# Two cross-attention layers: one after the other, or in common slots twelve tiles apart

## The chip, the cores and the metric

The kernel runs on one core of a Trainium2 chip. A core has a matrix engine (TensorE, PE in the profile; PEld is its weight load), a vector engine (VectorE, DVE), an engine for activation functions (ScalarE, ACT), a general engine (GpSimd, POOL) and a synchronization engine (SyncE, SP) that here issues all the DMAs. Each engine works through its own queue in order; semaphores make one engine wait for another. Operands lie in an on-chip memory of 128 partitions (SBUF), products of TensorE in a second one (PSUM). The metric is the device time of one execution in microseconds (us), the median of several runs.

## The reference

The input x has 4 batches of 1024 rows with 256 features; the context has 4 batches of 77 rows. Four layers follow each other. Layers 0 and 1 are the same in both kernels and are left out here. Layers 2 and 3 are attention from the rows of x to the 77 rows of the context, with 16 heads:

```python
# layer 2 (queries = x, keys = values = context)
q, k, v = heads(queries @ Wq.T + bq), heads(keys @ Wk.T + bk), heads(values @ Wv.T + bv)
scores = einsum('bhqd,bhkd->bhqk', q, k) / sqrt(16)
scores = where(attention_mask, -inf, scores * attention_weights)
out = einsum('bhqk,bhkd->bhqd', softmax(scores), v)
x = queries + heads_joined(out) @ Wo.T + bo
x = (x - mean(x)) * rsqrt(var(x) + 1e-5) * gamma + beta
# layer 3 (hidden_states = x, key_value_states = context)
normed = x * rsqrt(mean(x * x) + 1e-6) * norm_w
q, k, v = heads64(normed @ wq), heads64(context @ wk), heads64(context @ wv)
attn = softmax(einsum('bhqd,bhkd->bhqk', q, k))
x = x + heads64_joined(einsum('bhqk,bhkd->bhqd', attn, v)) @ wo
```

`attention_weights` and `attention_mask` are inputs of 4 x 16 x 1024 x 77, so that each tile of rows has its own. Layer 3 of a row needs layer 2 of that row alone: the rows do not mix in these two layers. All is float32.

## The kernel before, in words

x lies in SBUF for the whole kernel, as 4 batches (NB) of 8 tiles (NT) of 128 rows: 32 tiles. A row of scores has 16 heads x 77 keys = 1232 values (HK), or ten chunks of 128 columns (NC).

The order of the work is written out by hand: the program lists instructions, and each engine's queue holds its own in the order of the program. Software pipelining is therefore also written out: a *slot* i works on several tiles at once, each at a different step.

Layer 2, `slot2(i)` (line 1457), touches tile i and the tiles 1, 3, 4 and 5 before it. In order of the program: the sixteen exponentials of tile i-1 (ACT, L1473); the scores of tile i (PE, L51, `ps<-kb,qT`), their product with the attention weights (DVE, L1485) and the masked entries put to a low value (DVE, L1490); the output product of tile i-5 (PE, `po2`); the product of weights and values of tile i-4 (PE, `pvT`) and its copy `oT` (ACT, L1507); the maxima of tile i (DVE, L1510, scaled in L1514); the turning of the weights of tile i-3 (PE transposes, L1375, ten chunks in three groups, each followed by an ACT copy into `pT`, L1376); the addition of the output of tile i-5 to x (DVE, L1520; the bias on POOL, L1521); and last the sums of tile i-1 (DVE, L1526, L1527) and the division of its weights by them (POOL, L1528). The attention weights and the mask of tile i+1 are loaded into a `side` buffer, of which there are two, when slot i begins (SP, L1453, L1454).

Layer 3, `slot3(i)` (L1571), has its queries and keys folded into one matrix `G` per batch, and its values and output weights into one matrix `U` per batch, both computed much earlier and kept in DRAM. It touches tile i and tile i-2: in two halves, the turning of tile i-2 and the scores of tile i from `G` (PE), the maxima and the subtraction (DVE, L1599, L1600); then one exponential (ACT, L1608), the sums (DVE, L1611, L1612), the division (POOL, L1613); then the output of tile i-2 from `U` (PE), its addition to x (DVE, L1623) and its store (SP, L1624).

All 32 slots of layer 2 come first, then all 32 of layer 3; the five slots that empty the pipeline of layer 2 are laid into the first five of layer 3. Work that belongs to a batch and not to a tile runs as a *job*, a generator that is advanced a little at two places of each slot (`gap2`), by shares that `jobs2` and `jobs3` write down:

- `prep2(b)` makes the queries of layer 2: 16 transposes, copies, 16 products, biases.
- `norm2(b)` is the layer norm that ends layer 2: statistics (DVE), `inv_std` with a power on POOL (L293), the norm (ACT, L1543), gamma and beta (POOL, L1546, L1547).
- `stats3(b)` and `features3(b)` are the root-mean-square norm of layer 3: statistics, `inv_std`, the normed rows `xn` (DVE, L316), their transposes `ptx` (PE, L339) and `xT` (DVE, L345).
- `loads2(b)` loads the values `V` of layer 2, `loads3(b)` the matrices `G` (L1567) and `U` (L1398, L1401) of layer 3.
- `combine1` finishes the last batch of layer 1.

Buffers tie queues together: a load into a buffer waits until the last reader of what lay there is done, and it waits at the head of SP's queue, ahead of all the loads behind it. `U` and `V` share one pair of buffers, `pT` has three, the weights `s` have four, the PSUM pool for outputs (`po2`, `po3`) has one buffer, the small PSUM pool `sm` (transposes, values, query products) three, the pool for scores two.

Of the kernel before, what the change touches and what calls it, by code (L numbers as in the profile page):

```python
# [17 lines left out]
P = 128  # L18
# [9 lines left out]
SC = 0.25  # L28
# [3 lines left out]
def tile_xattn_seq(ctx: ExitStack, tc: tile.TileContext, d: dict, out: bass.AP):  # L32
# [252 lines left out]
    def inv_std(rs, mv, eps, rms):  # L285

        if rms:
            nc.gpsimd.tensor_tensor(rs, mv[:, :, 0], mv[:, :, 0], ALU.mult)
            nc.gpsimd.tensor_tensor(rs, rs, mv[:, :, 1], ALU.add)
            nc.gpsimd.tensor_scalar_add(rs, rs, eps)  # L290
        else:
            nc.gpsimd.tensor_scalar_add(rs, mv[:, :, 1], eps)
        nc.gpsimd.tensor_tensor(rs, rs, nhalf, ALU.pow)  # L293
# [1084 lines left out]
    def new_scores():  # L1378
        s = late.tile([P, P * NC], F32, name="s", tag="s", bufs=4)
        nc.gpsimd.memset(s[:, HK:], 0.0)  # L1380
        return s
# [11 lines left out]
    def load_folded(b):  # L1393

        U = late.tile([P, NC, D], F32, name="U3", tag="qu")
        rows_of_u = kept_u[b].rearrange("h s n -> (h s) n")
        n = P * (NC - 1)
        nc.sync.dma_start(  # L1398
            out=U[:, 0 : NC - 1, :], in_=rows_of_u[0:n].rearrange("(c p) n -> p c n", p=P)
        )  # L1400
        nc.sync.dma_start(out=U[0:HSIZE, NC - 1, :], in_=rows_of_u[n:HK])  # L1401
        return U

    def loads2(b):

        V = late.tile([P, NC, D], F32, name="V2", tag="qu").rearrange("p c n -> p (c n)")
        V = V[:, 0 : (NC + 1) * P].rearrange("p (c n) -> p c n", n=P)
# [18 lines left out]

    def prep2(b):

        x = xs[b]
        xT = late.tile([P, 2, T], F32, name="xT2", tag="xT")  # L1430
        yield from to_features(xT, lambda i: x[:, i, :], None, None, None, None)
        qT = late.tile([P, 2, T], F32, name="qT2", tag="gs")
        for o in range(2):
            for q in range(2):
                pp = sm.tile([P, 512], F32, name="pp2", tag="sm")
                for c in range(2):
                    mm(
                        pp, l2["Wq"][:, c, P * o : P * o + P], xT[:, c, 512 * q : 512 * q + 512],
# [6 lines left out]
                if o and q:  # L1445
                    shared["b2", b] = qT
                yield

    def load_sides(i):
        b, t = divmod(i, NT)  # L1450
        side = late.tile([P, HK + HK // 4], F32, name="side", tag="side")
# [5 lines left out]
    def slot2(i, tiles, at, gap2):  # L1457


        p1, p3, p4, p5 = (tiles.get(i - k) for k in (1, 3, 4, 5))  # L1460
        a = None
        if i < NB * NT:
            b, t = divmod(i, NT)
            a = tiles[i] = dict(b=b, t=t)
            qT, kb = shared["b2", b], shared["k2"]
            fs, mk = shared.pop(("side", i))
            if i + 1 < NB * NT:
                load_sides(i + 1)
            s = a["s"] = new_scores()
        if p1:  # L1470
            for h in range(H):
                hs = p1["s"][:, S * h : S * h + S]
                nc.scalar.activation(hs, hs, AF.Exp, bias=p1["nm"][:, h : h + 1], scale=SC)  # L1473
        if a:
            for o in range(2):
                ps = pair_tile()
                for e in range(2):
                    r = half_rows(e)
                    mm(
                        ps[:, e, 0 : 4 * S].rearrange("p (h s) -> p h s", s=S),  # L1480
                        qT[r, o, P * t : P * t + P],
                        kb[r, o, :, b, :],
                    )
                so = slice(o * HH * S, (o + 1) * HH * S)
                nc.vector.tensor_tensor(  # L1485
                    s[:, so].rearrange("p (i n) -> p i n", i=2), ps[:, :, 0 : 4 * S],
                    fs[:, so].rearrange("p (i n) -> p i n", i=2), ALU.mult,
                )
            sv = s[:, 0:HK]
            nc.vector.copy_predicated(sv, mk, low.to_broadcast([P, HK]))  # L1490
        gap2(at + 0.4)
        if p5:
            xt = xs[p5["b"]][:, p5["t"], :]
            po = pvp.tile([P, D], F32, name="po2", tag="pv")
            for o in range(2):
                mm(po, p5["oT"][:, o, :], l2["Wo"][:, o, :], start=(o == 0), stop=(o == 1))
            del tiles[i - 5]
        if p4:

            V = shared["v2", p4["b"]]  # L1500
            pv = sm.tile([P, 2, P], F32, name="pvT", tag="sm")
            for k in range(NC + 1):
                o, c = (0, k) if k < 5 else (1, k - 1)
                r = slice(0, rows_in(c))
                mm(pv[:, o, :], V[r, k, :], p4["pT"][r, c, :], start=k in (0, 5), stop=k in (4, NC))
            oT = p4["oT"] = late.tile([P, 2, P], F32, name="oT", tag="oT")
            nc.scalar.copy(oT, pv)  # L1507
        if a:
            nm = a["nm"] = small.tile([P, H], F32, name="nm", tag="m16")
            nc.vector.tensor_reduce(  # L1510
                nm, sv.rearrange("p (h k) -> p h k", k=S), axis=AX.X, op=ALU.max
            )

            nc.vector.tensor_scalar(nm, nm, 0.1 * NEG, -SC, ALU.max, ALU.mult)  # L1514
        if p3:
            pT = p3["pT"] = late.tile([P, NC, P], F32, name="pT", tag="pT", bufs=3)
            for g in range(3):
                turned(p3["s"], g, pT)
        if p5:
            nc.vector.tensor_tensor(xt, po, xt, ALU.add)  # L1520
            nc.gpsimd.tensor_tensor(xt, xt, rows["bo"], ALU.add)  # L1521
        gap2(at + 1.0)
        if p1:
            s3 = p1["s"][:, 0:HK].rearrange("p (h k) -> p h k", k=S)
            den = small.tile([P, H], F32, name="den", tag="den")
            nc.vector.tensor_reduce(den, s3, axis=AX.X, op=ALU.add)  # L1526
            nc.vector.reciprocal(den, den)  # L1527
            nc.gpsimd.tensor_tensor(  # L1528
                s3, s3, den.unsqueeze(2).to_broadcast([P, H, S]), ALU.mult
            )  # L1530

    def norm2(b):

        x = xs[b]
        res = []
        yield from stats_job(res, lambda t: x[:, t, :], 1e-5, False)
        mv, rs = res
        away = small.tile([P, NT], F32, name="away", tag="away")
        nc.gpsimd.tensor_tensor(away, mv[:, :, 0], rs, ALU.mult)
        nc.gpsimd.tensor_scalar(away, away, -1.0, None, ALU.mult)  # L1540
        for t in range(NT):
            xt = x[:, t, :]
            nc.scalar.activation(  # L1543
                xt, xt, AF.Identity, bias=away[:, t : t + 1], scale=rs[:, t : t + 1]
# [3 lines left out]
            yield  # L1548


    def stats3(b):

        res = shared["st3", b] = []
        yield from stats_job(res, lambda t: xs[b][:, t, :], 1e-6, True)

    def features3(b):

        xT = shared["xT3", b] = late.tile([P, 2, T], F32, name="xT3", tag="xT")
        rs = shared["st3", b][1]
        yield from to_features(  # L1560
            xT, lambda t: xs[b][:, t, :], None, rs, cols["L3_xattn_norm_w"], None
        )

    def loads3(b):

        G = late.tile([P, 2, 8, 2, S], F32, name="G3", tag="gs")
        nc.sync.dma_start(  # L1567
            out=G.rearrange("p c f e s -> p (c f e) s"),
            in_=kept_g.rearrange("p c f e (b s) -> p (c f e) b s", s=S)[:, :, b, :],
        )  # L1570
        shared["b3", b] = (G.rearrange("p c f e s -> p c (f e s)"), load_folded(b))  # L1571
        yield

    def slot3(i, tiles, at, gap2):
        a, p2 = None, tiles.get(i - 2)
        if i < NB * NT:
            b, t = divmod(i, NT)
            a = tiles[i] = dict(b=b, t=t)
            G, _ = shared["b3", b]
            xT = shared["xT3", b]  # L1580
            s = a["s"] = new_scores()
            m = small.tile([P, H], F32, name="m3", tag="m16")
        if p2:
            pT = late.tile([P, NC, P], F32, name="pT", tag="pT", bufs=3)
        for o in range(2):
            if p2:
                turned(p2["s"], o, pT)
            if a:
                ps = pair_tile()
                for e in range(2):  # L1590
                    k0 = (2 * o + e) * 4 * S
                    for c in range(2):
                        mm(
                            ps[:, e, 0 : 4 * S], xT[:, c, P * t : P * t + P],
                            G[:, c, k0 : k0 + 4 * S], start=(c == 0), stop=(c == 1),
                        )
                pv = ps[:, :, 0 : 4 * S].rearrange("p i (h s) -> p i h s", s=S)
                mo = m[:, HH * o : HH * o + HH].rearrange("p (i h) -> p i h", i=2)
                nc.vector.tensor_reduce(mo, pv, axis=AX.X, op=ALU.max)  # L1599
                nc.vector.tensor_tensor(  # L1600
# [271 lines left out]
```

## Time and profile before

| | |
|---|---|
| time, median of 3 runs | 2310.22 us (2309.99 to 2316.91) |
| profiled execution, its own time | 2315.16 us |
| span of the profiled execution | 2313.4 us |
| mean granted clock of TensorE | 0.981 |
| TensorE busy | 2167.0 us (94%) |
| VectorE busy | 1511.2 us (65%) |
| ScalarE busy | 1028.1 us (44%) |
| POOL busy | 642.4 us (28%) |
| first score of layer 2 | at 1723.3 us |
| first score of layer 3 | at 1982.3 us |

The profile is of one execution. An engine's busy time is the time in which it ran instructions; register and semaphore instructions and the issue of DMAs are not counted. A line of the timeline has a start, a length, the engine, the line of the kernel, the operation, the tile that is written and those that are read, the shapes, the number of equal instructions in a row, and in brackets how long the engine had been idle before and which engine and tile released it. All matrix products have line 51, that of a helper, so that they are told apart by their tiles. Products on TensorE overlap: the cost of one is better read from the distance to the next start than from its length. The clock that TensorE was granted stands as a part of full speed.

### The profile page before, as it was taken

The page shows a single profiled execution, that of the slowest core. Times are in us where ns is not written, and L with a number is a line of the kernel's source. Part 1 is how long each engine was busy: PE and PEld are TensorE (multiplying, and loading weights), DVE is VectorE, ACT ScalarE, POOL GpSimd, SP SyncE. Part 2 cuts the span into 40 slices and gives each one's busy share as a digit, 9 for nine tenths or more (in the row PEclk, how much of TensorE's full clock was granted, in tenths as well). Part 3 has the DMA queues.
Part 4 walks back from the last instruction along what each step waited for, and adds up shares of the span by engine and source line. Part 5 has one row for each costly group of instructions (what it writes and reads, how often), then busy time and mean ns, then how long its engine had stood idle before and what let it go on. Part 6 is the DMA issues. An engine that isn't in the chain of part 4 may idle for free.

```text
span 2313.4 us, 41275 instructions
## 1 busy us (share of the span) xinstructions
PE 2167.0 (94%) x16874; PEld 1357.5 (59%) x16874; DVE 1511.2 (65%) x2492; ACT 1028.1 (44%) x1700; POOL 642.4 (28%) x927
## 2 busy tenths in 40 slices
PE   4999999999999999999989999999999998999999
PEld 2544444555555455554556675656556776788887
DVE  3756567755566555754376666777759999677664
ACT  1144444434444444344533444545548876432222
POOL 2011113111131112310152232333423655542221
PEclk9899999999999999999989999999999999999999
DMA  7221121100000000101000011101023334102200
GB/s 216 55 57 68 32 64 41 40 6 15 7 15 2 10 11 6 38 1 19 6 15 6 15 28 19 21 15 21 15 78 124 114 109 126 47 15 58 58 14 17
DMA packets 87858, 93.98 MB, mean 41 GB/s; under 512 B 35714, under 2 KB 77558, under 8 KB 87542
## 3 DMA queue, kind: packets, MB, share of 16 engines
q1 hardware_dynamic: 87670, 91.35, 15.1%
q8 instruction: 133, 2.18, 0.4%
q14 instruction: 55, 0.45, 0.1%
HBM read 55.31 MB, written 18.39 MB: 32 GB/s over the span
## 4 chain that ended last, share of the span: by engine, by line
PE 70%; DVE 14%; ACT 5%; issue 1%; POOL 1%; DVEq 0%; ACTq 0%
PE ps L51 27%; PE po L51 13%; PE pv L51 6%; PE pp L51 6%; PE ph L51 4%; DVE mpart L672 3%; PE psT L1375 2%; DVE ms L1138 2%; PE ppv L51 2%; PE pvT L51 2%; PE pvw L51 1%; DVE mrow L1142 1%; PE ptx L339 1%; PE pm L590 1%; PE pt L607 1%
## 5 line engine op out<-in xcount | busy, mean ns | idle before, releaser
L51 PE MATMUL ps<-qk 32*128 32x192 f32 (+9 forms) x6528 | 581.9, 428 | 57.8 <-DVE mpart L672 25.0
L738 ACT ACTIVATE pe<-ps 128x1024 f32<-128x1024 f32 (+2 forms) x384 | 363.3, 952 | 589.5 <-PE ps L51 581.5
L51 PEld LDWEIGHTS ps<-qk 32*128 32x128 f32 (+1 forms) x6528 | 315.9, 185 | 295.8 <-issue 75.5
L672 DVE TENSOR_REDUCE mpart<-ps 128x2 f32<-128x1024 f32 (+4 forms) x384 | 330.9, 884 | 241.9 <-PE ps L51 241.2
L741 POOL TENSOR_SCALAR_AFFINE_SELECT pe<-pe 128x256 f32<-128x256 f32 (+1 forms) x192 | 94.9, 495 | 665.5 <-ACT pe L738 664.6
L1214 ACT ACTIVATE pew<-ps 128x768 f32<-128x768 f32 x128 | 103.4, 812 | 196.4 <-PE ps L51 196.3
L1219 POOL TENSOR_SCALAR_AFFINE_SELECT pew<-pew 128x512 f32<-128x512 f32 x128 | 81.7, 638 | 338.0 <-ACT pew L1214 337.9
L1376 ACT COPY pT<-psT 128x512 f32<-128x512 f32 (+1 forms) x192 | 92.3, 518 | 175.4 <-PE psT L1375 174.9
L1138 DVE TENSOR_TENSOR ms<-ps,maskw 128x768 f32<-128x768 f32 x128 | 122.1, 954 | 69.7 <-PE ps L51 68.2
L51 PE MATMUL pv<-pe,va 128*32 128x512 f32 (+3 forms) x1536 | 157.1, 496 | 0.0
L51 PE MATMUL ph<-yT,w 128*128 128x256 f32 x512 | 143.1, 401 | 2.4 <-DVE va L401 1.0
L51 PE MATMUL po<-U,pT 128*128 128x256 f32 (+1 forms) x640 | 143.7, 379 | 0.2
L51 PE MATMUL ps<-G,xT 128*128 128x308 f32 x512 | 143.0, 423 | 0.0
L51 PEld LDWEIGHTS po<-w,hT 128*128 128x128 f32 x800 | 111.6, 192 | 47.7 <-issue 38.9
L1473 ACT ACTIVATE s<-s,nm 128x77 f32<-128x77 f32 x512 | 131.2, 347 | 17.3 <-DVE nm L1514 17.2
L51 PE MATMUL po<-w,hT 128*128 128x128 f32 (+1 forms) x800 | 138.0, 317 | 0.9 <-ACT hT L904 0.9
L665 DVE TENSOR_REDUCE mpart<-ps 128x8 f32<-128x1024 f32 x64 | 78.2, 1225 | 82.6 <-PE ps L51 82.4
L1613 POOL TENSOR_TENSOR s<-s,den 128x1232 f32<-128x1232 f32 x32 | 71.9, 2248 | 203.4 <-DVE den L1612 176.9
L51 PEld LDWEIGHTS po<-U,pT 128*128 128x128 f32 (+1 forms) x640 | 119.2, 190 | 15.5 <-ACT pT L1376 0.6
L51 PEld LDWEIGHTS ph<-yT,w 128*128 128x128 f32 x512 | 88.7, 192 | 63.9 <-issue 50.8
L1142 DVE TENSOR_REDUCE mrow<-ms 128x4 f32<-128x768 f32 x128 | 122.2, 955 | 4.4
L1375 PE MATMUL psT<-ident,s 128*128 128x128 f32 x640 | 92.9, 274 | 16.8 <-ACT oT L1507 13.0
(200 smaller groups left out, 3381.9 us busy)
## 6 DMA issues: line engine op xcount, KB each, us to landing
side<-in_fside_t SPq DMA_DIRECT2D x32, 616.0 KB
qk<-st SPq DMA_DIRECT2D x256, 64.0 KB
side<-in_mask_t SPq DMA_DIRECT2D x32, 154.0 KB
G<-kept_g SPq DMA_DIRECT2D x4, 1232.0 KB
U<-kept_u SPq DMA_DIRECT2D x4, 1152.0 KB
x<-in_x SPq DMA_DIRECT2D x8, 512.0 KB
out<-x SPq DMA_DIRECT2D x32, 128.0 KB
kept_g<-st SPq DMA_DIRECT2D x22, 154.0 KB
```

What stands on the lines that cost most here:

```text
L51: nc.tensor.matmul(o, lhsT, rhs, start=start, stop=stop, **kw)
L665: nc.vector.tensor_reduce(mpart[self.own][:, :, 2 * p : 2 * p + 2, 0].rearrange("p t j -> p j t"), ps.rearrange("p j (t n) -> p j t n", n= ...
L672: nc.vector.tensor_reduce(mpart[bl][:, i, 2 * p : 2 * p + 2, ci], ps[:, :, o : o + w], axis=AX.X, op=ALU.max,)
L738: nc.scalar.activation(pp[:n, :, o:512], ps[:n, :, o:512], AF.Exp, scale=SC)
L741: nc.gpsimd.affine_select(out=own, in_=own, compare_op=ALU.is_ge, fill=0.0, base=0, pattern=[[0, 2], [0, k], [1, P]], channel_multiplier=-1,)
L1138: nc.vector.tensor_tensor(v, ps.rearrange("p j (i n) -> p j i n", i=2)[:, :, :, 0:n], (maskw[:, 1:2] if w else maskw).unsqueeze(1).to_broa ...
L1142: nc.vector.tensor_reduce(mo, v, axis=AX.X, op=ALU.max, negate=True)
L1214: nc.scalar.activation(pp[:, :, :, 0 : P + WIN], ps.rearrange("p j (i n) -> p j i n", i=2)[:, :, :, 0 : P + WIN], AF.Exp, scale=SC,)
L1219: nc.gpsimd.affine_select(out=pf[:, :, 0:P], in_=pf[:, :, 0:P], compare_op=ALU.is_ge, fill=0.0, base=0, pattern=[[0, 4], [1, P]], channel_ ...
L1375: nc.tensor.transpose(ps[:, k, :], s[:, P * c : P * c + P], ident)
L1376: nc.scalar.copy(pT[:, 4 * group : 4 * group + n, :], ps[:, 0:n, :])
L1473: nc.scalar.activation(hs, hs, AF.Exp, bias=p1["nm"][:, h : h + 1], scale=SC)
```

## The change

Layers 2 and 3 run in common slots. `slot23(i)` takes the place of `slot2` and `slot3`: slot i works on layer 2 of tile i and on layer 3 of tile i-12 (`LAG`). There are 46 slots: slots 0 to 11 have layer 2 alone, in the order that `slot2` had; slots 12 to 36 have both; slots 37 to 45 have layer 3 alone, in the order that `slot3` had, but for the sums and the division, which are issued one slot later, after the first half of the scores.

A common slot is ordered so (c: tile of layer 3, c1 and c2 the ones before; p1, p3, p4, p5: tiles of layer 2, one to five before): turning of c2; four exponentials of p1; scores of layer 2; sums and division of c1; four exponentials; `more()`; output of c2; four exponentials; maxima; values of p4; `more()`; the last four exponentials; scores of layer 3; `more()`; turning of p3; exponential of c; sums of p1; output of p5 and its addition; `more()`; division of p1.

`more()` takes the place of `gap2`: it advances every job that is alive by a fixed number of steps, one for `combine1` and `prep2`, two or four for `between`. `between(g)` takes the place of `norm2`, `stats3` and `features3`: for four tiles it runs the layer norm of layer 2, the root-mean-square statistics, the normed rows and their transposes, in some 20 steps. It starts at slot 9 + 4g. `prep2` works in two halves of 512 rows, its copies are on ACT, and `prep2(b+1)` starts in slot 8b + 4. `loads2(b+1)` and `loads3(b)` are issued, whole, ahead of slot 8b + 4.

Buffers: `G`, `U` and `V` have two each of their own; `pT` becomes `pT2` and `pT3` with one each; `s` becomes `s2` with four and `s3` with two; the queries, half the transposed rows and `xT3` take places of weights that are no longer used.

The core of the diff, with the jobs:

```diff
-    def slot2(i, tiles, at, gap2):
-    def slot3(i, tiles, at, gap2):
...
+    def turned_x(dst, rows, g):
+
+        for c in range(2):
+            pt = sm.tile([P, 4, P], F32, name="ptx", tag="sm")
+            for i in range(4):
+                nc.tensor.transpose(pt[:, i, :], rows[i][:, c * P : (c + 1) * P], ident)
+            src = pt.rearrange("p i n -> p (i n)")
+            if g is None:
+                nc.scalar.copy(dst[:, c, :], src)
+            else:
+                nc.vector.tensor_scalar(dst[:, c, :], src, g[:, c : c + 1], None, ALU.mult)
+            yield
+
...
+    def stats4(st, mv, rs, g, eps, rms):
+
+        b, t0 = divmod(4 * g, NT)
+        for k in range(4):
+            nc.vector.bn_stats(st[:, k], xs[b][:, t0 + k, :])
+            nc.vector.bn_aggr(mv[:, k], st[:, k])
+            if k == 3:
+                inv_std(rs, mv, eps, rms)
+            yield
+        yield
+
+    def between(g):
+        b, t0 = divmod(4 * g, NT)
+        x = xs[b]
...
+        yield from stats4(st, mv, rs, g, 1e-5, False)
+        away = late.tile([P, 4], F32, name="away", tag="away")
+        nc.gpsimd.tensor_tensor(away, mv[:, :, 0], rs, ALU.mult)
+        nc.gpsimd.tensor_scalar(away, away, -1.0, None, ALU.mult)
+        yield
+        for k in range(4):
+            xt = x[:, t0 + k, :]
+            nc.scalar.activation(
+                xt, xt, AF.Identity, bias=away[:, k : k + 1], scale=rs[:, k : k + 1]
+            )
+            nc.gpsimd.tensor_tensor(xt, xt, rows["gamma"], ALU.mult)
+            nc.gpsimd.tensor_tensor(xt, xt, rows["beta"], ALU.add)
+            yield
...
+        yield from stats4(st, mv, rs, g, 1e-6, True)
+        xn = []
+        for k in range(4):
+            xt = small.tile([P, D], F32, name="xn", tag="xn", bufs=4)
+            normed(xt, x[:, t0 + k, :], None, rs, k)
+            xn.append(xt)
+            if k % 2:
+                yield
+        xT = shared["xT3"][:, g % 2]
+        yield from turned_x(xT, xn, cols["L3_xattn_norm_w"])
+        shared["ready3"] = g
+
+    LAG = 12
...
+        elif i < n + 5:
+            if c2:
+                turned_into(c2, "pT3")
+            if p1:
+                exps2(p1, range(4))
+            if a:
+                score2(a, i)
+            if c1:
+                sums_of(c1, "den3")
+                divided(c1)
+            if p1:
+                exps2(p1, range(4, 8))
+            more()
+            if c2:
+                out3(c2)
+            if p1:
+                exps2(p1, range(8, 12))
+            if a:
+                maxima2(a)
+            if p4:
+                values_of2(p4)
+            more()
+            if p1:
+                exps2(p1, range(12, H))
+            if c:
+                score3(c, j)
+            more()
+            if p3:
+                turned_into(p3, "pT2")
+            if c:
+                exp3(c)
+            if p1:
+                sums_of(p1, "den2")
+            if p5:
+                out2(p5)
+                add2(p5)
+            more()
+            if p1:
+                divided(p1)
...
-    run(slots(slot3, 2, jobs3, slots(slot2, 5, jobs2)))
...
+    for i in range(NB * NT + LAG + 2):
+        b, k = divmod(i, NT)
...
+        if k == 4:
+            if b + 1 < NB:
+                run(loads2(b + 1))
+            if b < NB:
+                run(loads3(b))
+        if k == 4 and b + 1 < NB:
+            live2.append((prep2(b + 1), 1))
+        if i >= 9 and (i - 9) % 4 == 0 and (i - 9) // 4 < NB * NT // 4:
+            live2.append((between((i - 9) // 4), 2 if i < 33 else 4))
+        slot23(i, two, three, more)
```

## The prediction

> **What bounds the kernel now.** I read the chain that ended last first (TensorE 70% of it), then the busy time by stage from the first score of layer 2 (1723.3 us) to the end, where all of the change lies: 590.1 us. Columns: window, its length, busy time (and instructions) per engine, granted clock, DMA share, GB/s.
>
> ```profile
> core 0: us, PE busy (x) PEld busy (x) DVE busy (x) ACT busy (x) POOL busy (x), PEclk, DMA share, GB/s
> 1723.30:1810.20 86.90, 79.45 (x504) 59.42 (x504) 82.92 (x106) 67.18 (x226) 28.90 (x29) 1.00 0.36 117
> 1810.20:1982.30 172.10, 149.28 (x964) 118.95 (x963) 157.86 (x239) 133.39 (x445) 105.81 (x126) 0.92 0.34 106
> 1982.30:2313.40 331.10, 325.83 (x1624) 267.19 (x1622) 210.88 (x330) 97.03 (x148) 101.56 (x103) 1.00 0.13 36
> ```
>
> Layer 2 (first two rows) is held by VectorE (157.9 of 172.1), layer 3 by TensorE (325.8 of 331.1). That is what common slots could use: together the stages ask 554.6 of TensorE, 451.7 of VectorE. So at best 590.1 − 554.6 = 35.5 us can be won. Next, the pitch of a tile, from starts of POOL's divisions (start, length):
>
> ```profile
> 1773.89 2.25 POOL L1528 TENSOR_TENSOR s<-s,den 128x1232 f32<-128x1232 f32 x1 [0.96 <-DVE den L1527]
> 1780.55 2.25 POOL L1528 TENSOR_TENSOR s<-s,den 128x1232 f32<-128x1232 f32 x1 [0.97 <-DVE den L1527]
> ...
> 2289.50 2.25 POOL L1613 TENSOR_TENSOR s<-s,den 128x1232 f32<-128x1232 f32 x1 [7.24 <-DVE den L1612]
> 2299.07 2.25 POOL L1613 TENSOR_TENSOR s<-s,den 128x1232 f32<-128x1232 f32 x1 [7.24 <-DVE den L1612]
> ```
>
> A slot of layer 2 with no job takes 6.65, one of layer 3 9.57 (6.65 is VectorE's work, 9.57 TensorE's). TensorE's work comes from the distances of starts in its timeline:
>
> ```profile
> 1771.19 1.31 PE L51 MATMUL ps<-kb,qT 64*128 64x308 f32 x8
> 1772.43 1.13 PE L51 MATMUL po<-w2q,oT 128*128 128x256 f32 x4
> 1773.40 2.62 PE L51 MATMUL pvT<-pT,V 128*128 128x128 f32 x22
> 1775.85 1.26 PE L1375 MATMUL psT<-ident,s 128*128 128x128 f32 x10
> ...
> 2104.09 2.24 PE L51 MATMUL ps<-G,xT 128*128 128x308 f32 x8
> ...
> 2108.90 4.49 PE L51 MATMUL po<-U,pT 128*128 128x256 f32 x20
> ```
>
> Layer 2: scores 1.05, output .86, values 2.45, turning 1.08 = 5.45 (each less what the next overlaps). Layer 3: scores 4.15, output 4.33, turning 1.08 = 9.56. A common slot costs TensorE 15.0. VectorE: 6.65 + 5.25 (max, subtract, sums, add) + a quarter of `between` (eight statistics of .53, four normed rows of .3, two `xT` of .75 = 7.0 per four tiles) = 13.7. So TensorE would be the bound of an undisturbed common slot, by 1.3 us.
>
> **What a late producer costs.** Waits of TensorE in layer 2 (total, times, longest), then one of them and the clock behind it:
>
> ```profile
> PE psT L1375 <- ACT oT L1507: 13.0, 6, 4.2
> PE ptx L339 <- DVE xn L316: 2.7, 2, 2.5
> ```
> ```profile
> 1833.83 0.69 PE L1375 MATMUL psT<-ident,s 128*128 128x128 f32 x2 [4.12 <-ACT oT L1507]
> 1834.45 2.42 PE L51 MATMUL ps<-kb,qT 64*128 64x308 f32 x8
> ```
> ```profile
> 1832.00:1833.80 1.80, 0.00 (x0) 0.50 0.63 244
> 1837.00:1838.00 1.00, 1.00 (x3) 0.50 0.00 0
> 1839.00:1840.00 1.00, 1.00 (x12) 1.00 0.00 0
> ```
>
> After 4.1 us without work the clock stood at .50 until about 1838.6; the scores took 2.42 instead of 1.31. From 1833.8 on that is 4.8 us at half speed: 2.4 lost beside the wait itself. The Trainium skill ("TensorE: Matmul & The Clock Gate", Part 1, the HAM clock gate) puts the return to full clock after about 3.4 us of sustained activity, which would make it an estimated 1.7 per episode and 5 us off the sum below; the row shows longer, and the row is taken.
>
> ```profile
> 2104.29 2.68 DVE L316 TENSOR_SCALAR xn<-x,rs 128x256 f32<-128x256 f32 x2
> 2110.43 0.61 DVE L316 TENSOR_SCALAR xn<-x,rs 128x256 f32<-128x256 f32 x2
> ```
>
> The same pair of normed rows took .61 alone, and 2.68 while POOL divided.
>
> **The change part by part.** From 1723.3, each piece to the next, at TensorE's costs unless said.
>
> Start: `prep2(0)` in two halves, one more round of transposes, copy and product: +.8 (0 to 2).
>
> Slots 0–11, layer 2 alone, 12 × 6.65 = 79.8, less 3.3 for the first slots, which lack exponentials and products. Added: layer 1's last combining 2.7 (as before); `prep2(1)`'s 8.7 of TensorE (16 transposes 1.8, 16 products × .43) no longer spread over the batch but in slots 4 and 5: 2 × 5.45 − .86 + 8.7 = 18.7 against VectorE's 13.3, +5.4 (0 to 8.7). SP issues V, G and U (3 MB; G ran at about 260 GB/s, U at 400) ahead of the side load for tile 5: some 15 us until it lands, the product of slot 5 waits, +4 (0 to 9). `between(0)` runs in slots 9–11 on the bound engine: 7.0 + POOL's chain for the second `rs` (three small operations .9, power 1.67) 2.6 + one blocked pair 2.1 = 11.7 (7 to 14). Sum 100.3; before, 86.9.
>
> Slots 12, 13 to the end of layer 3's second score: 2 × 9.6, less 1.9 that follows that score, + 5.3 of `prep2(2)`: 22.6.
>
> Slots 14–31: 18 × 15.03 = 270.5; rest of `prep2(2)` and all of `prep2(3)` 12.1; five pairs of `ptx` groups .86 = 4.3; ScalarE's norms stand ahead of the copies of `pT3`, 5 × 1.05 = 5.3 (0 to 8). Then three waits:
>
> (1) In the third slot of each `between` (15, 19, 23, 27, 31) TensorE's order is second score, `ptx` transposes, output of layer 3. VectorE issues before the last two normed rows: statistics of two tiles, sums of p1, add, first two rows, two products, predicated copy, sums of c1. From the end of the score of layer 3, TensorE is ready at 1.08 + .86 + 1.08 + 1.05 = 4.1. VectorE, in ends since that score (subtract .8 a half, statistics .53 a tile, sums 1.44 + .25, products 1.44, predicated copy 1.61, from their rows): subtract 1.7, statistics 2.8, sums 4.4, add 4.75, `rs` from POOL at 5.4, first rows 6.1 (8.2 blocked), products, copy and sums + 4.73, last rows: 11.6 free, 16.5 with both pairs blocked. Wait 7.5 to 12.4; without the `rs` wait and at best order 5.3. No gain is possible from a wait. I take 9.0, between free and blocked, since the divisions of the slot cover about half: 45. VectorE's 1.3 spare cannot make it good, as the bound engine itself stands still. Queued behind: everything on TensorE.
>
> The Trainium skill ("SBUF — State Buffer", Who interferes with whom) says that whichever of VectorE's two-port operations or GpSimd issues second is blocked for the whole instruction, which speaks against the change, since two divisions now lie in each slot. With every pair blocked the sum would be 17 us higher; the rows show blocked and free pairs side by side, so the middle stays.
>
> (2) These waits exceed 4.1, so each halves the clock: 5 × 2.4 = 12 (0 to 12).
>
> (3) At slots 20 and 28 `loads3` stands in SP's queue ahead of the side load of tile 21 (29). U waits for its buffer: the last output product of tile 7 (15), in slot 21 (29). That ends 8.5 after the score; issue 1.2, U 3.3, side 1.6 + 2 landing: the product finds its side at about 15.7 instead of 3.9; VectorE, then TensorE, wait. I take 9 each (0 if half of it is made up behind, 13 if landing is slower): 18.
>
> Sum 367.2.
>
> Slots 32–36 (layer 2 running out): 3 × 13.95 + 12.9 + 10.4 = 65.1; `ptx` .9, wait at slot 34 7.0, clock 2.4: 75.4. Slots 37–43: 7 × 9.57 = 67; `ptx` .9, wait at 39 5.8, clock 2.4: 76.1. End: last score to end 19.5, as now (2294.0 to 2313.4).
>
> .8 + 100.3 + 22.6 + 367.2 + 75.4 + 76.1 + 19.5 = 661.9, +71.8 against 590.1. The profiled execution took 2315.16 (span 2313.4), 4.94 above the median of the runs, 2310.22. So 2387 on its scale, 2382 as a median. Costed at nothing: POOL's divisions issued last (3 of 15 us, TensorE covers them; without cover 2.25 a slot), the output DMAs, memsets of .14.
>
> **The rivals.** *The transposes find their rows ready* (other side). Place: slots 15 to 39; price 45 + 7 + 5.8 and clock 16.8 = 74.6 off: 587.3, so 2307. It decides if the wait falls below about 1 us a group, VectorE having run a slot ahead. For it: 1.3 us spare per slot, `ptx` waited only 2.7 in all before. Against: the five steps behind each slot's own score can't start earlier. With the side loads also in time, 569: 2289.
>
> *VectorE becomes the bound*: blocked rows and `nm` scaling beside two divisions, 1 us over 15.0 in 25 slots: 2407. For: 157.9 of 172.1 in layer 2. Against: 1.3 spare.
>
> *Small waits*: (1) at 5.3, (3) at 5, no clock loss, tile 5's side in time: −18.5 − 8 − 17 − 4: 2335.
>
> **How the numbers follow.** Forecast .68 (2345 to 2410); VectorE-bound or slower DMA .13 (2400 to 2440); small waits .07 (2317 to 2340); ready transposes .12, of it .05 within 0.3% and .07 faster. 0.3% (7 us) is about what a measurement here tells from no change. Low 2335 is the sum of small waits. High: (1) at 12.4 (+17), (3) at 13 (+8), half of the VectorE case (+18): 2425. Outside are .12 + .03 below and .04 above.
>
> **What would show it.** TensorE idle before `ptx` (line 1437), releaser VectorE's `xn`, seven times 5 to 12 us, clock .5 behind; SP's U issue late and VectorE's product (1545) waiting for a DMA at slots 21 and 29; POOL waits in slots 9–11; 9.57 in slots 37–43. Wrong, if common slots pass 15.5 without such a wait, or `ptx` idles under 2 us.

## The result, and the profile after

The changed kernel takes 2406.5 us (median of 4 runs, 2401.64 to 2412.32) against 2312.22 in the same comparison: ratio 1.0406, 95% interval 1.0376 to 1.0436. It is 94 us slower. The forecast was 2382, with a range of 2335 to 2425.

The profiled execution has a span of 2404.9 us. Layers 0 and 1 are the same code in every kernel here, yet the first score of layer 2 starts at 1723.3 us before and at 1725.4 after, and between 1720.1 and 1728.1 over all profiled executions of this study. Stages are therefore compared from that score to the end: 590.1 us before, 679.5 after.

Busy times of the changed kernel, cut where the prediction cut its sum (columns: window, length, busy time and instructions of each engine, granted clock, DMA share, GB/s):

```profile
core 0: us, PE busy (x) PEld busy (x) DVE busy (x) ACT busy (x) POOL busy (x), PEclk, DMA share, GB/s
1725.37:1832.21 106.84, 81.80 (x479) 62.99 (x479) 85.05 (x114) 68.06 (x227) 36.76 (x44) 0.87 0.36 112
1832.21:1857.00 24.79, 23.33 (x131) 17.36 (x131) 16.24 (x20) 15.37 (x46) 6.50 (x9) 1.00 0.71 199
1857.00:2227.70 370.70, 315.35 (x1702) 253.91 (x1702) 259.98 (x384) 161.16 (x462) 144.45 (x173) 0.91 0.19 58
2227.70:2306.85 79.15, 70.81 (x388) 59.85 (x386) 37.61 (x66) 24.77 (x56) 28.80 (x33) 0.96 0.03 9
2306.85:2384.27 77.42, 68.10 (x314) 53.55 (x313) 40.49 (x68) 20.79 (x31) 24.00 (x29) 0.96 0.03 11
2384.27:2404.90 20.63, 16.28 (x83) 13.50 (x81) 6.81 (x10) 4.30 (x8) 4.63 (x3) 0.96 0.06 19
```

The third row is the heart: in the slots with both layers neither TensorE (315 of 371) nor VectorE (260) is full, and the clock is .91. An average like this says that engines wait for each other, and the waits say where. TensorE's, and then VectorE's (total, times, longest):

```profile
PE ptx L1437 <- DVE xn L316: 57.4, 21, 5.5
PE ps L51 <- DVE s L1545: 13.6, 3, 6.2
```
```profile
DVE s L1545 <- DMA side<-in_fside_t: 47.8, 4, 16.6
DVE s L1627 <- PE psT L1375: 11.9, 6, 2.0
DVE s L1545 <- DMA side<-in_mask_t: 10.1, 1, 10.1
```

Before, TensorE waited 2.7 us in all for `xn`. One of the five slots with the transposes (slot 19), first VectorE, then TensorE:

```profile
1955.39 0.36 DVE L1602 TENSOR_TENSOR x<-po,x 128x256 f32<-128x256 f32 x1
1955.90 3.14 DVE L316 TENSOR_SCALAR xn<-x,rs 128x256 f32<-128x256 f32 x2
1958.96 1.49 DVE L1545 TENSOR_TENSOR s<-ps,side 128x616 f32<-128x616 f32 x2
1960.48 1.58 DVE L1550 COPY_PREDICATED_SCALAR s<-side,low 128x1232 f32 x1
1961.95 1.42 DVE L1567 TENSOR_REDUCE den<-s 128x16 f32<-128x1232 f32 x1
1963.40 0.25 DVE L1570 RECIPROCAL den<-den 128x16 f32<-128x16 f32 x1
1963.57 0.52 DVE L316 TENSOR_SCALAR xn<-x,rs 128x256 f32<-128x256 f32 x2
```
```profile
1954.09 1.31 PE L51 MATMUL ps<-kb,qT 64*128 64x308 f32 x8
1956.85 0.30 PE L1437 MATMUL ptx<-ident,xn 128*128 128x128 f32 x1 [1.45 <-DVE xn L316]
1959.09 0.33 PE L1437 MATMUL ptx<-ident,xn 128*128 128x128 f32 x1 [1.94 <-DVE xn L316]
1963.89 0.73 PE L1437 MATMUL ptx<-ident,xn 128*128 128x128 f32 x2 [4.47 <-DVE xn L316]
1964.42 7.18 PE L51 MATMUL po<-U,pT 128*128 128x256 f32 x20
```

TensorE is through with the scores at 1955.4 and wants the four normed rows; VectorE makes two of them, then four other steps, then the other two. TensorE stands for 7.9 us, and the output product behind takes 7.18 instead of 4.49. The first pair of rows took 3.14 beside a division of POOL, the second, free, .52. Layer 3's score follows that of the slot before by 27.5 us (1946.80 to 1974.33), in slots without these transposes and without a piece of `prep2` by 15.4 to 15.7.

SP in slot 21, and VectorE's wait behind it:

```profile
2007.80 0.38 SPq L1403 DMA_DIRECT2D U<-kept_u  x1
2008.23 0.59 SPq L1406 DMA_DIRECT2D U<-kept_u  x1
2008.87 0.42 SPq L1474 DMA_DIRECT2D side<-in_fside_t  x1
```
```profile
2015.75 1.51 DVE L1545 TENSOR_TENSOR s<-ps,side 128x616 f32<-128x616 f32 x2 [16.61 <-DMA side<-in_fside_t]
```

U goes out when the last output product of tile 7 is done, the side load for tile 21 behind it, though slot 20 had asked for it; VectorE stood still for 16.6 us and its whole queue with it.

### The profile page after: what moved, and what is told of

It reads as the page before. It is cut to its first block, busy times and chain, and to the rows that moved or that the text cites. A ratio compares the mean times of both kernels' runs of the same rounds, so it can differ in the third digit from the quotient of the medians.

```text
span 2404.9 us, 41135 instructions
## 1 busy us (share of the span) xinstructions
PE 2182.6 (91%) x16842; PEld 1372.7 (57%) x16874; DVE 1503.7 (63%) x2476; ACT 1026.4 (43%) x1716; POOL 650.8 (27%) x959
## 4 chain that ended last, share of the span: by engine, by line
PE 65%; DVE 15%; ACT 4%; POOL 2%; issue 2%; DMA 2%; SPq 1%; DVEq 0%; POOLq 0%; ACTq 0%
PE ps L51 25%; PE po L51 12%; PE pv L51 6%; PE pp L51 4%; PE ph L51 4%; DVE mpart L672 3%; PE pvT L51 2%; DVE ms L1138 2%; PE ppv L51 2%; PE psT L1375 2%; DMA side<-in_fside_t 1%; PE pvw L51 1%; DVE den L1567 1%; DVE mrow L1142 1%; PE pm L590 1%
## 5 line engine op out<-in xcount | busy, mean ns | idle before, releaser
L1574 POOL TENSOR_TENSOR s<-s,den 128x1232 f32<-128x1232 f32 x64 | 145.0, 2266 | 145.4 <-DVE den L1570 145.4
L51 PE MATMUL po<-U,pT 128*128 128x256 f32 (+1 forms) x640 | 159.3, 408 | 6.0 <-ACT pT L1376 4.5
L51 PEld LDWEIGHTS po<-U,pT 128*128 128x128 f32 (+1 forms) x640 | 130.0, 207 | 31.2 <-ACT pT L1376 12.2
L51 PEld LDWEIGHTS ps<-G,xT 128*128 128x128 f32 x512 | 97.4, 196 | 46.5 <-DVE s L1545 14.3
```

The costliest lines, as they stand in the source:

```text
L51: nc.tensor.matmul(o, lhsT, rhs, start=start, stop=stop, **kw)
L1574: nc.gpsimd.tensor_tensor(s3, s3, a["den"].unsqueeze(2).to_broadcast([P, H, S]), ALU.mult)
```

## The experiments

The theory is that of the prediction: the losses are places where a queue in order stands at an instruction whose input is late, and not a lack of engine time. The rivals are that VectorE is the bound of common slots, so that a wait taken away comes back elsewhere, and that loads and clock cost nothing of their own. Where single microseconds count, the stage (first score of layer 2 to the end, in the profiled execution) is given beside the ratio, since layers 0 and 1 vary by more; it rests on one profile of each kernel. The kernel before, run again beside each group, had medians of 2312.2 to 2317.1, so that gains over the changed kernel come out 2 to 4 us larger by the ratios than by the medians.

### The transposes of `between` later

```diff
         for k in range(4):
             ...
+        for _ in range(3):
+            yield
         xT = shared["xT3"][:, g % 2]
         yield from turned_x(xT, xn, cols["L3_xattn_norm_w"])
```

> Only the two groups of ptx transposes move, three steps of between later: behind the scores of layer 3 of the same slot. Theory (TensorE's queue stands at transposes whose rows VectorE makes late): the waits on xn go (57.4 us in the profile after, 50 of them in the common slots), and the halved clock behind each with them, about 2.7 us in seven places, so 60 to 75 us less than the changed kernel: 2330 to 2345. Rival (common slots are bound by VectorE or its lock with POOL, and the wait only shows at ptx): the wait comes back at another tile of TensorE's queue, and less than 25 us are won: over 2380.

Measured: 2348.54, 58 us less than the changed kernel; ratio to the kernel before 1.0137 (1.0122 to 1.0152); stage 621.4. The same slot 19, TensorE:

```profile
1949.79 4.05 PE L51 MATMUL ps<-G,xT 128*128 128x308 f32 x15
1953.68 1.04 PE L1437 MATMUL ptx<-ident,xn 128*128 128x128 f32 x8
1954.55 0.60 PE L1375 MATMUL psT<-ident,s 128*128 128x128 f32 x4
1955.88 0.66 PE L1375 MATMUL psT<-ident,s 128*128 128x128 f32 x4 [0.73 <-ACT pT L1376]
1956.82 0.44 PE L1375 MATMUL psT<-ident,s 128*128 128x128 f32 x2 [0.28 <-DVE xT L1442]
```

The wait for `xn` is gone from the common slots (4.7 us are left in the stage, in slots of one layer), and from layer 3's score in slot 18 to that in slot 20 it takes 34.5 us (1933.59 to 1968.09) instead of 43.8 (1946.80 to 1990.57). Of each gain some 1.0 is lost again to new waits, as both groups now lie together ahead of the turning and the small PSUM pool has three buffers. So the theory holds and the rival falls: VectorE does the same work in the shorter slot. The gain, 58 by medians and stage and 62 by the ratios, is at or just under the low end of the 60 to 75 expected: the expectation left these new waits out.

### The loads of layer 3 two slots later

```diff
         if k == 4:
             if b + 1 < NB:
                 run(loads2(b + 1))
-            if b < NB:
-                run(loads3(b))
+        if k == 6 and b < NB:
+            run(loads3(b))
```

> Only loads3 (G and U) is issued two slots later, in slots 6, 14, 22 and 30, when U's buffer is already free. Theory (SP stands at U, and the side load behind it comes late): VectorE's waits for the side load of 16.6 us at slots 21 and 29 go, and those of slots 5 and 13 shrink by half, since G and U no longer lie ahead: 25 to 35 us less than the changed kernel, 2371 to 2382. Rival (the loads are hidden, and the time at slots 21 and 29 is that of prep2's products, which crowd into two slots): less than 8 us won, 2398 or more.

Measured: 2376.39, 30 us less; ratio 1.0258 (1.0243 to 1.0273); stage 648.7. Of VectorE's four waits for the first half of the side load, 47.8 us, one of 3.3 in slot 5 is left, where `V` still lies ahead; the one of 10.1 for the mask, which ends at the first product of the stage, stays at the same size as after. By distances of layer 3's scores: from slot 20 to 22 47.4 became 39.0, from slot 28 to 30 42.4 became 31.1, and from the first score of layer 2 to layer 3's in slot 14 148.4 became 139.3. That is 8.4 + 11.3 + 9.1 = 28.8 of the 30.8 of the stage. The rival, the products of `prep2`, falls: they are still in these slots. They do show: VectorE now waits 16.8 us for scores of layer 2 (4.4 after), but the 30.8 are won all the same.

### Both

> Both edits together. If the two losses are separate, as the theory has it, the gains add: 85 to 110 us less than the changed kernel, 2297 to 2322, level with the kernel before. If one wait had hidden the other, the sum is smaller than its parts by 15 us or more.

Measured: 2317.68; ratio 1.0004 (.9994 to 1.0014), the same time as the kernel before; stage 589.9. The stage is 89.6 shorter than after; the parts were 58.1 and 30.8, together 88.9. The two losses are separate and add.

### Score buffers for the slots of layer 3 alone

In VectorE's list after, `s L1627` waiting for `psT` (11.9 us, six times) is the subtraction that may not write its buffer before the tile two back is turned.

```diff
-            a["s"] = new_scores("s3", 2)
+            a["s"] = new_scores(*(("s3", 2) if j < NB * NT - 7 else ("s2", 4)))
```

> Both edits, and the weights of layer 3 take the four buffers of layer 2 from slot 37 on, when these are no longer used. In the profile after a slot of layer 3 alone takes 10.43 us, not 9.57: the subtraction of VectorE waits 2.0 for the turning of the tile two before (there are two buffers s3), the sums behind it come late, and the next turning waits .65 for POOL's division. Theory (buffers): slots 38 to 43 go back to 9.6, 5 us less than with both edits. Rival (the sums issued a slot later are late by their place in VectorE's queue): the slot stays at 10.4, and no time is won.

Measured: 2307.77; ratio .9961 (.9946 to .9975), stage 584.5, 5.4 less than with both edits alone (the medians of the runs differ by 9.9, of which layers 0 and 1 can make some). The turning of two slots, with two buffers (the kernel with both edits) and with four:

```profile
2279.34 0.66 PE L1375 MATMUL psT<-ident,s 128*128 128x128 f32 x4 [0.65 <-POOL s L1576]
...
2289.77 0.66 PE L1375 MATMUL psT<-ident,s 128*128 128x128 f32 x4 [0.65 <-POOL s L1576]
```
```profile
2270.49 0.60 PE L1375 MATMUL psT<-ident,s 128*128 128x128 f32 x4
...
2280.06 0.60 PE L1375 MATMUL psT<-ident,s 128*128 128x128 f32 x4
```

10.43 became 9.57. The sums are issued in the same place in both, so it is the buffer and not the place.

### The division of p1 not last

```diff
             if p1:
                 sums_of(p1, "den2")
+                divided(p1)
             if p5:
                 out2(p5)
                 add2(p5)
             more()
-            if p1:
-                divided(p1)
```

> On top of both edits and the free score buffers: in a common slot POOL's division of p1 is issued right behind its sums and no longer last, ahead of the bias of p5 and of between's gamma, beta and powers. The prediction costed the place at nothing (POOL is busy a third of the slot, and the turning of p1 comes two slots later): within 4 us of the version before. Rival (the place matters: bias and norm, which the next slot's statistics wait for, come 2.25 us later, and normed rows meet the division): 5 to 15 us slower.

Measured: 2309.17; ratio .9972 (.9959 to .9986); stage 584.8 against 584.5. The place of the division makes no difference that these runs can tell, as the prediction had it.

### The idle time of TensorE filled

This kernel is the changed one with empty work in the wait; the rest of its computation is whole.

```diff
             for i in range(4):
+                if g is not None and c == 0 and i == 2:
+                    for _ in range(30):
+                        nc.tensor.transpose(pt[:, 3, :], ident, ident)
                 nc.tensor.transpose(pt[:, i, :], rows[i][:, c * P : (c + 1) * P], ident)
```

> The changed kernel as it was, with 30 transposes of the unit matrix laid between the second and the third row of the first ptx group of each between, into the place that the fourth row's transpose then writes over: some 3.3 us of empty work, inside the wait of 4.5 that is there in any case. No wait is taken away; only the idle time of TensorE is cut into pieces of under 2 us. Theory (an idle stretch of over 4 us halves the clock and costs 2.4 to 2.7 more behind it): output products behind ptx take 4.5 and not 7.2, six or seven times: 13 to 19 us less than the changed kernel, 2388 to 2394. Rival (the clock's loss lies where TensorE waits anyway, or empties add to the queue): within 4 us, or slower.

Measured: 2394.79, 12 us less than the changed kernel though TensorE does more; ratio 1.0346 (1.0322 to 1.037); stage 668.9, 10.6 less. Slot 19, and the clock in it (window, length, busy time, clock):

```profile
1958.43 0.33 PE L1440 MATMUL ptx<-ident,xn 128*128 128x128 f32 x1 [1.94 <-DVE xn L316]
1958.59 5.10 PE L1439 MATMUL ptx<-ident 128*128 128x128 f32 x30
1963.53 0.38 PE L1440 MATMUL ptx<-ident,xn 128*128 128x128 f32 x2
1963.75 4.48 PE L51 MATMUL po<-U,pT 128*128 128x256 f32 x20
```
```profile
1956.60:1958.30 1.70, 0.00 (x0) 1.00 0.00 0
1958.60:1960.00 1.40, 1.40 (x11) 0.73 0.00 0
1960.00:1961.00 1.00, 1.00 (x7) 0.50 0.00 0
1962.00:1963.00 1.00, 1.00 (x8) 0.67 0.00 0
1963.80:1965.00 1.20, 1.20 (x8) 1.00 0.00 0
```

The output product takes 4.48 instead of 7.18. The clock still fell, but its slow stretch now lies over empty work inside the wait. The five common slots with transposes are 1.5 to 2.7 us shorter, 11.3 in all (slots 15, 19, 23, 27 and 31). So the halved clock is a loss of its own beside the wait, of some 2.3 us a place there. In slot 34 only .4 is won, as the empty work there ends 1.6 us late, and in slot 39 the output product behind stays at 6.17. The gain, 12 us by medians, 14 by the ratios and 10.6 by the stage, is at or under the low end of the 13 to 19 expected.

### Four steps towards a faster kernel

From the version with both edits and free score buffers on. The queries spread over four slots:

```diff
+            if len(e) > 2:
+                e[2] += 1
+                each = e[2] % 2 + (e[2] == 16)
...
-            live2.append((prep2(b + 1), 1))
+            live2.append([prep2(b + 1), 1, 0])
```

> On top of both edits and the free score buffers: prep2 takes a step at every second more(), so that its 8 pieces fill slots 4 to 7 of each batch and not 4 and 5. Theory (slots 4 and 5 are bound by TensorE with 4.4 of query products in each, the others before and after by VectorE): VectorE's waits for the scores of slots 5 and 6 of 4.9 and 3.7 us go, 5 to 8 us less than the version before, 2300 to 2303; in common slots nothing, as TensorE is the bound there. Rival (the L2 slots only hand the wait on): within 3 us.

Measured: ratio .9968 (.9955 to .998), no better than .9961; stage 581.4, 3.1 less. The 5 to 8 us of the theory are not there; the rival's 3 fit. A wait of 3.3 ahead of a turning in slot 4 is in both versions, with POOL's memset as its releaser before and ScalarE's copy `xT` after.

The two `ptx` groups at two places (`range(4)` in the first experiment's edit, with the spread):

> As with the spread queries, and the two ptx groups at two places: one behind the score of layer 3, one behind the output of layer 2. With both at one place the turning behind them waits .73 for a copy of pT and .29 for xT in each of five slots, since the small PSUM pool has three buffers. Theory: these waits go, 3 to 5 us less than with the spread alone. Rival: ScalarE's copies are late anyway, nothing is won.

Measured: 2306.48; ratio .9959 (.9946 to .9971); stage 579.3, 2.1 less than with the spread alone, where 3 to 5 were expected.

All of `between` begun three of four places earlier, which also shifts its last slots (the 3 is a count of places of `more()` that the job lets pass):

```diff
-        if i >= 9 and (i - 9) % 4 == 0 and (i - 9) // 4 < NB * NT // 4:
-            live2.append((between((i - 9) // 4), 2 if i < 33 else 4))
+        if i >= 8 and i % 4 == 0 and (i - 8) // 4 < NB * NT // 4:
+            live2.append([between((i - 8) // 4), 2 if i < 32 else 4, None, 3])
```

> On top of the spread queries and split ptx: every between begins three of the four places earlier, at the end of slot 8 + 4g, right behind the addition that it needs. In the version before, ScalarE's first two norms of between(0) stand in its queue ahead of the copy oT of slot 10 and wait for POOL's power; TensorE waits 4.2 us behind, its clock halves, and ptx of slot 11 waits 2.6 more. Theory: these waits and the halved clock behind them go, 6 to 10 us less, 2297 to 2301. Rival (VectorE is the bound of slots 9 to 11 and sets their pace whatever TensorE waits for): within 3 us of the version before.

Measured: ratio .9969 (.9957 to .998); stage 580.8, no gain. Up to the first score of layer 3 3.9 us are won (98.8 instead of 102.7 from the first score of layer 2), and lost again near the end of layer 2, where four steps a place bring the old wait back:

```profile
2181.92 1.24 PE L1437 MATMUL ptx<-ident,xn 128*128 128x128 f32 x3 [5.19 <-DVE xn L316]
```

And the addition of p5 ahead of the sums of p1, on the version with spread and split:

```diff
-            if p1:
-                sums_of(p1, "den2")
             if p5:
                 out2(p5)
                 add2(p5)
+            if p1:
+                sums_of(p1, "den2")
```

> On top of the spread queries and split ptx (the earlier start of between is left out again): in a common slot the addition of p5 is issued ahead of the sums of p1. The single PSUM buffer of the outputs is free for layer 3's output only when VectorE has read layer 2's, and VectorE does so behind the sums (1.67 us): TensorE waits .5 there in eight or nine slots, 4 us in all. Theory: these waits go, 3 to 4 us less from the first score of layer 2 to the end (575 to 576 against 579.3), a ratio to the kernel before of about .994. Rival (sums and division that come .4 later are waited for instead): no gain.

Measured: 2305.23 (2300.12 to 2308.57); ratio .9953 (.9938 to .9968); stage 578.4, .9 less where 3 to 4 were expected. The waits for the addition went from 3.8 to 1.6 us, those for copies of `pT` rose by 1.5: most of the gain comes back at another wait, though not at the sums and the division, which the rival named. It is the fastest version here by its median, 0.5% under the kernel before; the intervals of the four last versions overlap, so that their order among themselves is not settled.

## Why the prediction was right

Piece by piece, forecast against the changed kernel's stage, whose sum is 679.5 for 661.1 forecast (without the .8 ahead of the first score):

| piece | forecast | measured |
|---|---|---|
| slots 0–11 | 100.3 | 106.8 |
| slots 12, 13 | 22.6 | 24.8 |
| slots 14–31 | 367.2 | 370.7 |
| slots 32–36 | 75.4 | 79.2 |
| slots 37–43 | 76.1 | 77.4 |
| end | 19.5 | 20.6 |

*The direction and its mechanism* were right: TensorE stands at `ptx`, in the seven places forecast and in slot 11, which was not, and SP at U. With both taken out the kernel is level with the one before, so these two are the loss. The rival of the other side, transposes whose rows are ready, did not come about; made by hand, it gives back 58 of its 74.6: the seven waits were 50.1 us and not 57.8, the clock behind them took about 14 and not 16.8, the move itself brings 5 us of new waits, and a wait of 2.1 is left in slot 39.

*Slots 0 to 11* hold the step that was mis-sized most. Up to the score of slot 9 the forecast adds up to 68.7 and 68.2 were measured; slots 9 to 11, three slots of 6.65 and 11.7 for `between(0)`, were 38.6 for 31.7. The term was costed on VectorE and POOL alone, and TensorE's waits there were put at nothing:

```profile
1812.91 0.69 PE L1375 MATMUL psT<-ident,s 128*128 128x128 f32 x2 [4.23 <-ACT oT L1593]
...
1820.47 0.66 PE L1437 MATMUL ptx<-ident,xn 128*128 128x128 f32 x2 [4.51 <-DVE xn L316]
1823.89 0.74 PE L1437 MATMUL ptx<-ident,xn 128*128 128x128 f32 x2 [2.76 <-DVE xn L316]
```

The clock stood at .50 from 1812.8 to 1829.9, so that the output and value products behind them took 1.91 and 4.43 us instead of 1.03 and 2.62. With the transposes later (the first experiment) the three slots take 31.9 us, as forecast; 2.2 of the 6.7 won come back in slot 12.

*Term (1)*, 9.0 for each wait in slots 15 to 31, measured 7.7 to 7.9: first pair blocked, second free, as "between free and blocked" had it. Its two ends do not follow from its own terms: 6.1 + 4.73 + .61 is 11.4 and 8.2 + 4.73 + 2.68 is 15.6, so that the wait runs from 7.3 to 11.5. The waits at slots 34 and 39 (7.0 and 5.8 forecast) were 4.9 and 6.1.

*Term (2)*, 2.4 for the clock: 1.3 to 2.7 by the output products behind the seven waits, which took 5.76 to 7.18 us instead of 4.49, 14.1 in all; 2.3 as a mean of what filling the idle time gave in five of them. The row of the kernel before was a good price. The estimate of 1.7 from the Trainium skill ("TensorE: Matmul & The Clock Gate", Part 1, the HAM clock gate) fits slots 15 and 23, where filling won 1.7 and 1.5, and was too low for slots 19, 27 and 31, where it won 2.7 each.

*Term (3)*, 9 each at slots 21 and 29: 8.4 and 11.3 by the loads moved, sum 19.7 for 18. That it is so near is in part luck: its own parts add up to 16.6 where it says 15.7, and some 2.3 and 3.1 of the loss are the halved clock behind the wait (the score products of layer 3 took 6.61 and 7.39 us instead of 4.31), which the term did not hold.

*The side load behind V, G and U*, +4 at slot 5: with G and U out of its way the stretch up to the score of slot 9 is 4.2 shorter. VectorE waited 11.5 there, and the same queue at slot 13 (a wait of 6.6) was not priced at all; it cost 3.5 in slots 13 and 14.

*Slots 14 to 31* came out near by terms that cancel: the five waits were 6 us less, the slot without any wait 15.4 and not 15.0, some 7 us in 18 slots, and slot 14 had 1.9 of the unpriced load. In slots 32 to 36 four waits of TensorE, for the one output buffer (.67, .68) and for copies of `pT` (.49, 1.56), were put at nothing; they are 3.4 us.

*Slots 37 to 43* were forecast at 9.57 and were 10.43, because the change in buffers, two for `s3` instead of four for all, was not followed: VectorE may not overwrite a tile that is not yet turned, and the sums behind it reach POOL late. The buffer experiment measured it at 5.4 us of stage. The total of the piece came out near because seven full slots were counted where six distances and 5.9 us at the two ends were run, five of 10.4 and one, with the transposes, of 19.4.

*VectorE becomes the bound* did not come: common slots without transposes or pieces of `prep2` kept 15.4 to 15.7 for 15.0 forecast, with VectorE at 260 of 371. The high end of the range counts half of this rival as 18 us, where half of its 25 is 12.5; with the ends of term (1) as added up above the range would have ended near 2415.

## What to carry to other kernels

Room on two engines is not yet a gain: an overlap that had at best 35 us to offer cost 89 here, because one late producer holds a whole queue in order. For each instruction that a change moves, list what the producing engine issues ahead of it and what the consuming engine has behind it; the wait read off that list was right within 17% in the five common slots here, the place that was not listed (slot 11) cost nearly as much as one of them, and moving the consumer behind the next score took the waits away. Do the same for loads, whose queue is easily forgotten, and for buffer counts: a transfer that waits for its buffer holds all transfers behind it, and a buffer fewer is a wait more.

## What the runs showed of the hardware that was not expected

The clock fell after short pieces of idle time, not after one long one. In slot 19 of the changed kernel TensorE was idle for 1.45 and 1.94 us, with a lone transpose of .3 us behind each, and then for 4.47 us (window, length, busy time, clock):

```profile
1957.20:1959.00 1.80, 0.00 (x0) 1.00 0.03 9
1959.50:1961.00 1.50, 0.00 (x0) 0.54 0.00 0
...
1968.00:1969.00 1.00, 1.00 (x4) 0.50 0.00 0
1969.00:1970.00 1.00, 1.00 (x4) 0.57 0.00 0
1970.00:1971.00 1.00, 1.00 (x6) 1.00 0.00 0
```

It was down from about 1959.6, some 4.2 us after the scores ended at 1955.4, with two lone transposes in between that did not keep it up, and came back near 1969.9, 6 us after steady work had begun at 1963.9. Where the idle time was filled, it came back about 4 us after the empty work had begun (1958.6 to 1962.7).

What decides between 4 and 6 was not tried, but the profiles hold more. The slow stretch lasted 10.24 us in the changed kernel and 3.41 where the time was filled, and in the clock records of all twelve profiles every stretch at one clock, full or half, lasts a whole multiple of 3.41 us (the first and the last of an execution apart). So the clock changed only on a grid of 3.41 us, and how much work fell into a slow stretch depended on where in the grid it began: 3.9, 6.0, 3.5, 5.8 and 5.9 us in slots 15, 19, 23, 27 and 31, where filling the idle time won 1.7, 2.7, 1.5, 2.7 and 2.7. How busy a step must be for the clock to stay up is not shown.
